# Down projection by seven products of half matrices in place of eight

## The chip, the cores and the metric

The kernel runs on one core of a Trainium2 chip. Five engines work side by side, each with an instruction queue of its own that it works off in order: PE (TensorE, matmuls), DVE (VectorE), ACT (ScalarE), POOL (GpSimd) and SP (SyncE, which here only issues DMAs). All data are f32. The metric is the device time of one execution in microseconds (us), median of three runs.

## The reference

The input x is 8 sequences of 512 tokens with 512 features. After a layer norm two branches run on each sequence. The first is a state space model (input projection, causal convolution of four taps, a scan with 16 states over 1024 channels, gating, output projection). The second is a gated feed-forward network whose gate is shifted by a low-rank term that an attention yields. The output is x + s * silu(g). What the change touches is the end of the second branch:

```python
gate_pre = h @ W_in_base.T + mod * (h @ A) @ B
gate = jax.nn.silu(gate_pre)
up = h @ W_up_base.T
mlp_out = gate * up @ W_down.T          # (512 x 2048) @ (2048 x 512), per sequence
return residual + mlp_out
```

The residual is the normalised x.

## The kernel before

**Two stages.** The first 640 us are the attention of all eight sequences (32 items: 8 sequences x 4 groups of heads). An order written out as a string of letters places each step; a table `const_steps` hangs small extra steps at given places (sequence, group, slot) of it. After that comes the scan stage, one sequence ("batch") after another, in which everything else happens: for batch b the scan, gate/up projections, down projection and z gates, for batch b - 1 the output projection, for batch b + 1 the input projection and convolution.

**The scan loop.** A batch has 64 iterations k, each with two chunks. An iteration holds a tile x of 128 x 1024 (two states of a channel block). It is loaded ahead by SP (`load_scan(k + 5)`, L650), multiplied by the input factor (`inputs`: on DVE for even k, L672, on POOL for odd k, L674), scanned in two halves on DVE (`scan_half`, L680, with the decays that ACT writes to PSUM, L658), multiplied by the output factor on POOL (`outputs`, L685), and summed over the states on PE (`sum_states`, L697, a burst of 16 instructions every four iterations).

**The work beside it.** The PE work of a batch is a list of parts (`batch_parts`), each with a number of units (one unit is a 512-column f32 matmul, which is two instructions), the weight tiles that it needs, and a function. `prefetch` has SP load weights up to `limits` minus one tiles ahead. In each chunk parts are issued until the share of units done has reached the share of chunks done. A part returns functions with a delay in chunks; `next_chunk` calls those that are due before the scan half of that chunk, and so they stand in DVE's, ACT's or POOL's queue at that place. The total is 300 units per batch.

**PSUM banks.** `bank` hands out four banks for matmul results in turn, two of a pool `ps_1` and two of a second pool.

**The down projection** stands last in the list of a batch, with z gates (`z_gate`, eight per batch) spread between. `down_proj(b, m)` makes output block m (128 features x 512 tokens) as one accumulation of 16 matmuls (L372) of 512 columns: the operand is `mlp[b, f]` (128 hidden features x 512 tokens), the weights are four tiles of 256 KB (`load_down`, L240). One chunk after its last part DVE adds the residual (L379, from the PSUM bank), ACT writes the tanh back to the bank (L380), and one chunk later DVE makes tanh and sum into twice the silu (L385, one input in PSUM). After the first block's parts `load_h(b + 1)` is issued: five DMAs on SP that bring the next batch's h into the tile `ht`, which has one buffer, and its modulation.

**What makes the operand.** `gate_up` computes four hidden blocks at a time (fq of 0 to 3, block 4 fq + i): gate (L310, L340) and then up, whose product with the gate (`up(i)`, L345) is the finished `mlp` tile. The first eight blocks are those of fq 0 and 1.

**The step size of the next batch** is a chain of small operations on DVE and ACT (`exponential`, `logarithm`, `softplus`, `scaled`, L556 to L594) that falls into the same stretch as the down projection.

Of the kernel before, what the change touches and what calls it, by code (L numbers as in the profile page):

```python
# [10 lines left out]
F32 = mybir.dt.float32  # L11
BF16 = mybir.dt.bfloat16
AF = mybir.ActivationFunctionType
ALU = mybir.AluOpType
# [4 lines left out]
P = 128  # L19
NB = 8  # L20
S = 512
DM = 512
KT = DM // P
TT = S // P
DI = 1024
ND = DI // P
# [3 lines left out]
HG = NH * HD // P  # L30
NF = 2048 // P
# [5 lines left out]
QD = 32  # L37
AHEAD = 5
SLOTS = TT * (TT + 1) // 2


@with_exitstack
def mamba_gated_ffn_kernel(
# [31 lines left out]
    scr_m = [dram.tile([R, S], F32, tag=f"scr_m{b}", name=f"scr_m{b}") for b in range(NB)]  # L75
    scr_c = [dram.tile([DI, S], F32, tag=f"scr_c{b}", name=f"scr_c{b}") for b in range(NB)]
    scr_r = [dram.tile([S], F32, tag=f"scr_r{b}", name=f"scr_r{b}") for b in range(NB)]
    scr_a = dram.tile([NS, P // NS, P], F32, tag="scr_a", name="scr_a")

    ident = const.tile([P, P], F32, tag="ident", name="ident")  # L80
# [12 lines left out]
    ctx.enter_context(tc.manual_schedule())  # L93


    banks = {"n": 0, "second": None, "special": None}

    def bank(name):
        if banks["special"]:
            return banks["special"](name)  # L100
        banks["n"] += 1
        pool = banks["second"] if banks["second"] and banks["n"] % 4 // 2 else ps_1
        return pool.tile([P, 512], F32, tag="mm", name=name)

    xnt, ht = {}, {}
# [5 lines left out]
    def load_h(b):  # L111
        ht[b] = act.tile([P, KT, S], F32, tag="ht", name=f"ht_{b}", bufs=1)
        nc.sync.dma_start(ht[b], scr_x[b][:, KT:, :])
        modh[b] = act.tile([4 * QD, S], F32, tag="modh", name=f"modh_{b}", bufs=1)
        for i in range(4):
            nc.sync.dma_start(modh[b][i * QD : i * QD + R, :], scr_m[b])
# [118 lines left out]
        nc.sync.dma_start(w, w_ffn[f][:, which])  # L235
        loaded["wgu", b, f, which] = w

    def load_down(b, m, q):
        w = wst.tile([P, NF // 4, P], F32, tag="wd", name=f"wd_{b}_{m}_{q}", bufs=4)
        nc.sync.dma_start(w, w_ffn[ts(q, NF // 4), :, 2, m, :].rearrange("f p c -> p f c"))  # L240
        loaded["wd", b, m, q] = w

    def load_out(b, m, q):
        w = wst.tile([P, ND // 2, P], F32, tag="wout", name=f"wout_{b}_{m}_{q}", bufs=3)
# [55 lines left out]
    def gate_up(b, fq):  # L300
# [42 lines left out]
        def up(i):  # L343
            m = mlp[b, 4 * fq + i]
            nc.vector.scalar_tensor_tensor(m, m, 0.5, st[i, 1], ALU.mult, ALU.mult)  # L345

        def second(i):
            product(i, 1, range(KT))
            return [(2, lambda: up(i))]

        def part(i, which, units, fn):
            p = units, [("wgu", lambda: load_gu(b, 4 * fq + i, which))], fn
# [6 lines left out]

    silus = {}  # L360

    def down_proj(b, m):

        st = {}

        def down(q):
            if q == 0:
                st["acc"] = bank(f"ps_acc_{b}_{m}")
            w = loaded.pop(("wd", b, m, q))
            for j in range(NF // 4):  # L370
                f = q * (NF // 4) + j
                nc.tensor.matmul(  # L372
                    st["acc"], lhsT=w[:, j, :], rhs=mlp[b, f], start=(f == 0), stop=(f == NF - 1)
                )
            return [(1, residual), (2, product)] if q == 3 else []

        def residual():
            f = tmp.tile([P, S], F32, tag="f", name=f"f_{b}_{m}", bufs=KT + 1)
            nc.vector.tensor_tensor(f, st["acc"], xnt[b][:, m, :], ALU.add)  # L379
            nc.scalar.activation(st["acc"], f, AF.Tanh, scale=0.5)  # L380
            st["f"] = f

        def product():
            f = st["f"]
            nc.vector.scalar_tensor_tensor(f, st["acc"], 1.0, f, ALU.add, ALU.mult)  # L385
            silus[b, m] = f

        return [
            (4, [("wd", lambda q=q: load_down(b, m, q))], lambda q=q: down(q)) for q in range(4)
        ]  # L390

    def finish(b, m):
# [45 lines left out]
    def finish_last(b, m):  # L438

        st = {}  # L440
        H = S // 2

        def out_proj(h, blocks):
            if "ps" not in st:
# [267 lines left out]
    def batch_parts(b):  # L712
# [23 lines left out]
        else:  # L736
# [1 line left out]
                parts += quads[i][0] + convs[2 * i] + quads[i][1][:2] + convs[2 * i + 1]  # L738
                parts += quads[i][1][2:]
            parts += sizes[0]  # L740
        for m in range(KT):
            down = down_proj(b, m)
            parts += down
            if m == 0 and b + 1 < NB:
                parts.append((0, [], lambda: load_h(b + 1)))
        total = sum(p[0] for p in parts) + 4 * ND
        done, out_, z = 0, [], 0
        for p in parts:
# [48 lines left out]
    with ExitStack() as c1:  # L797
# [272 lines left out]
        def turn(b, kt):  # L1070

            if kt == 0:
                xnT[b] = act.tile([P, KT, S], F32, tag="ht", name=f"xnT_{b}", bufs=1)
                xrT[b] = act.tile([P, KT, S], F32, tag="xnt", name=f"xrT_{b}")
            ps = bank(f"ps_x_{b}_{kt}")
            for tt in range(TT):
                nc.tensor.transpose(ps[:, ts(tt, P)], norm[b][tt][:, ts(kt, P)], ident)

            def evict():
                nc.scalar.copy(xnT[b][:, kt, :], ps)  # L1080
                nc.gpsimd.tensor_tensor(  # L1081
                    xrT[b][:, kt, :].rearrange("p (t c) -> p t c", t=TT),
                    xnT[b][:, kt, :].rearrange("p (t c) -> p t c", t=TT),
                    rms[b][1].rearrange("p (c t) -> p t c", t=TT), ALU.mult,
                )
                if kt == KT - 1:
                    nc.sync.dma_start(scr_x[b][:, :KT, :], xnT[b])

            return evict
# [213 lines left out]
        def started(parts):  # L1303
# [14 lines left out]
            [],  # L1318
        )

        const_steps = dict(zip(
            ((0, 0, 3), (0, 1, 2), (1, 0, 0), (1, 0, 1), (1, 1, 0), (1, 1, 1), (1, 1, 2), (1, 2, 1),
             (1, 2, 2)),
            constants(),
        ))
        sizes = step_size(0)

        spare = {}

# [323 lines left out]
```

## Time and profile before

Before: 2956.67 us, median of three runs (2955.38 to 2958.57).

| what | us |
|---|---|
| profiled execution | 2959.42 |
| its span, first to last instruction | 2957.6 |
| PE busy | 2916.1 |
| DVE busy | 2508.3 |
| POOL busy | 1983.2 |
| matmuls of the down projection (L372), 1024 instructions | 451.3 |
| scans on DVE (L680), 1024 | 1208.5 |
| output factor on POOL (L685), 512 | 1206.6 |
| granted PE clock, mean | 0.997 |

A group's line gives line, engine, operation, output <- inputs, shapes and count, then busy us and the mean ns of one, then the idle time of the engine before it and what ended it. PEld is the loading of weights, which runs beside PE's matmuls. A line of the chain gives the share of the span in which a line's work was what the end waited for. A line of stretches gives from:to, its length, then busy us and count of PE, PEld, DVE, ACT and POOL, the granted clock, the share of DMA and GB/s. A line of the timeline gives start, length, engine, line, operation.

### The profile page before, as it was taken

How to read it: one execution, taken by the hardware profiler on the slowest of the kernel's cores; microseconds unless marked ns; L12 is line 12 of the kernel's file. 1: busy time of each engine (PE TensorE's matmuls, PEld its weight loads, DVE VectorE, ACT ScalarE, POOL GpSimd, SP SyncE). 2: the span in 40 equal slices, each digit the busy share in tenths (PEclk: the TensorE clock that was granted, in tenths of full speed). 3: DMA queues.
4: the chain of work that ended last, by engine and by line, in shares of the span. 5: the costliest groups of instructions: out<-in, count | busy, mean ns of one | idle time of the engine just before them, and what ended most of it. 6: DMA issues, size and time to landing. Idle time of an engine off the chain costs nothing.

```text
span 2957.6 us, 33937 instructions
## 1 busy us (share of the span) xinstructions
PE 2916.1 (99%) x11440; PEld 1257.8 (43%) x11440; DVE 2508.3 (85%) x2855; ACT 1258.7 (43%) x2192; POOL 1983.2 (67%) x924
## 2 busy tenths in 40 slices
PE   9999999999999999999999999999999999999999
PEld 5544545444333443444444344434443444344434
DVE  5777777688998999799979987998799879988885
ACT  4555555443444344334433433443344334433332
POOL 3433333107889778777878777777778777878884
PEclk9999999999999999999999999999999999999999
DMA  4767777779887978797879787877787878788874
GB/s 162 196 188 192 194 194 195 202 201 220 213 198 204 236 202 204 201 232 195 201 197 230 198 202 193 231 202 203 187 234 187 208 186 241 190 209 200 209 195 114
DMA packets 316465, 595.00 MB, mean 201 GB/s; under 512 B 32605, under 2 KB 164317, under 8 KB 311684
## 3 DMA queue, kind: packets, MB, share of 16 engines
q1 hardware_dynamic: 310096, 576.31, 75.2%
q0 software_dynamic: 2192, 10.50, 1.0%
q10 hardware_dynamic: 4004, 6.01, 0.8%
q8 instruction: 92, 1.51, 0.2%
q14 instruction: 81, 0.66, 0.1%
HBM read 466.04 MB, written 42.77 MB: 172 GB/s over the span
## 4 chain that ended last, share of the span: by engine, by line
PE 90%; DVE 5%; ACT 1%; SPq 1%; DMA 1%; POOL 1%; issue 1%; DVEq 0%; POOLq 0%; ACTq 0%
PE ps_gu L310 30%; PE ps_acc L372 15%; PE ps_in L218 13%; PE y L697 8%; PE ps_out L401 7%; PE ps_q L1136 3%; PE s L1159 2%; PE ps_k L1136 2%; PE o_ps L1220 2%; DVE mx L1172 2%; DVE p L1196 1%; PE ps_z L1113 1%; PE ps_gu L321 1%; SPq L1205 1%; ACT p L1181 1%; PE s L1164 1%
## 5 line engine op out<-in xcount | busy, mean ns | idle before, releaser
L685 POOL TENSOR_TENSOR x<-x,cc 128x1024 f32<-128x1024 f32 x512 | 1206.6, 2364 | 451.6 <-DVE x L680 425.9
L680 DVE TENSOR_TENSOR_SCAN x<-decay,x 128x512 f32<-128x512 f32 x1024 | 1208.5, 1208 | 3.0 <-ACT decay L658 2.7
L658 ACT ACTIVATE decay<-dt,an 128x511 f32<-128x511 f32 x1024 | 695.3, 687 | 643.9 <-DVE x L680 627.0
L310 PE MATMUL ps_gu<-ht,wgu 128*128 128x512 f32 x2048 | 914.8, 598 | 0.0
L674 POOL TENSOR_TENSOR x<-x,bb 128x1024 f32<-128x1024 f32 x256 | 607.5, 2373 | 67.2 <-DMA wgu<-in_w_ffn 64.9
L310 PEld LDWEIGHTS ps_gu<-ht,wgu 128*128 128x128 f32 x2048 | 381.0, 190 | 521.7 <-issue 475.6
L372 PE MATMUL ps_acc<-m,wd 128*128 128x512 f32 x1024 | 451.3, 597 | 0.0
L218 PE MATMUL ps_in<-xnt,win 128*128 128x512 f32 x952 | 426.2, 594 | 0.0
L1181 ACT ACTIVATE p<-s,mx 128x256 f32<-128x256 f32 (+3 forms) x512 | 228.3, 528 | 193.7 <-DVE mx L1172 185.7
L672 DVE TENSOR_TENSOR x<-x,dtb_ps 128x1024 f32<-128x1024 f32 x255 | 304.6, 1194 | 1.1 <-ACT dtb_ps L669 0.5
L372 PEld LDWEIGHTS ps_acc<-m,wd 128*128 128x128 f32 x1024 | 192.2, 190 | 259.0 <-issue 250.8
L218 PEld LDWEIGHTS ps_in<-xnt,win 128*128 128x128 f32 x952 | 178.2, 190 | 221.5 <-issue 215.0
L1172 DVE TENSOR_REDUCE mx<-s 128x2 f32<-128x1024 f32 (+3 forms) x256 | 196.5, 808 | 76.0 <-PE s L1164 76.0
L697 PE MATMUL y<-x,sel 128*32 128x512 f32 x2048 | 251.2, 601 | 4.8 <-POOL x L685 4.8
L401 PE MATMUL ps_out<-xc,wout 128*128 128x512 f32 x496 | 219.4, 594 | 0.0
L1196 DVE STREAM_TRANSPOSE p<-p 128x2048 f32<-128x2048 f32 (+3 forms) x128 | 188.7, 1493 | 23.9 <-ACT p L1181 21.4
L257 DVE SCALAR_TENSOR_TENSOR conv<-ps_in,cw,conv 128x511 f32<-128x511 f32 x165 | 122.8, 745 | 42.2 <-ACT conv L276 38.3
L401 PEld LDWEIGHTS ps_out<-xc,wout 128*128 128x128 f32 x496 | 92.7, 190 | 118.8 <-issue 118.8
L1081 POOL TENSOR_TENSOR xrT<-xnT,rms 128x512 f32<-128x512 f32 x28 | 42.9, 1532 | 141.7 <-ACT xnT L1080 141.7
L1159 PE MATMUL s<-k,q 32*128 32x512 f32 (+3 forms) x1024 | 123.3, 480 | 8.8 <-ACT p L1181 8.0
L294 ACT ACTIVATE zth<-ps_in 128x512 f32<-128x512 f32 x64 | 38.2, 597 | 220.0 <-PE ps_in L218 220.0
L697 PEld LDWEIGHTS y<-x,sel 128*32 128x32 f32 x2048 | 54.3, 109 | 181.2 <-issue 145.5
(214 smaller groups left out, 2103.7 us busy)
## 6 DMA issues: line engine op xcount, KB each, us to landing
x<-scr_c SPq DMA_DIRECT2D x512, 512.0 KB, 6.7
pt<-p SPq DMA_DIRECT2D x512, 160.0 KB, 3.4
wgu<-in_w_ffn SPq DMA_DIRECT2D x256, 256.0 KB, 5.7
win<-in_w_in SPq DMA_DIRECT2D x128, 256.0 KB, 5.3
wd<-in_w_ffn SPq DMA_DIRECT2D x128, 256.0 KB, 5.1
scr_c<-xc SPq DMA_DIRECT2D x64, 256.0 KB, 3.7
wout<-in_out_w SPq DMA_DIRECT2D x64, 256.0 KB, 4.3
xt<-in_x SPq DMA_DIRECT2D x32, 256.0 KB, 4.3
```

The source lines that it names most:

```text
L218: nc.tensor.matmul(ps, lhsT=w[:, kt, :], rhs=xnt[b][:, kt, :], start=(kt == 0), stop=(kt == KT - 1))
L310: nc.tensor.matmul(st[i, which], lhsT=w[:, kt, :], rhs=ht[b][:, kt, :], start=(kt == 0), stop=(kt == KT - 1 and (which == 1 or i == 3)),)
L372: nc.tensor.matmul(st["acc"], lhsT=w[:, j, :], rhs=mlp[b, f], start=(f == 0), stop=(f == NF - 1))
L401: nc.tensor.matmul(st["ps"], lhsT=w[:, d % 4, :], rhs=xc[b, d], start=(d == 0), stop=(d == ND - 1),)
L658: nc.scalar.activation(decay[n][:, 1:], spread[b][2][:, 1:], AF.Exp, scale=an[:, g // 4, g % 4 : g % 4 + 1])
L672: nc.vector.tensor_tensor(t, t, by.unsqueeze(1).to_broadcast([P, 2, S]), ALU.mult)
L674: nc.gpsimd.tensor_tensor(t, t, spread[b][0].unsqueeze(1).to_broadcast([P, 2, S]), ALU.mult)
L680: nc.vector.tensor_tensor_scan(t, decay[n], t, 0.0, ALU.mult, ALU.add)
L685: nc.gpsimd.tensor_tensor(t, t, spread[b][1].unsqueeze(1).to_broadcast([P, 2, S]), ALU.mult)
L697: nc.tensor.matmul(y[ts(j, QD), :], lhsT=sel[:, i0 + n, :], rhs=xs[k - 3 + j][:, n, :], start=(i0 + n == 0), stop=(i0 + n == 3),)
L1172: nc.vector.reduce_max(mx[i], sc[i][:, :, :w], axis=AX.X, negate=True)
L1181: nc.scalar.activation(to[:, :, :, ts(h, QD)].rearrange("p b k i -> p k b i"), sc[h // 2][:, h % 2, :w].rearrange("p (k b i) -> p k b i", ...
```

## The change

The operand of the down projection (2048 hidden features x 512 tokens) and the weights are cut in halves both ways: hidden features into low (blocks 0 to 7) and high (8 to 15), tokens into FIRST and SECOND (256 each), output features into two pairs of blocks. The eight products of quarters become seven (Strassen's algorithm in the form with shared sums), in the order 1, 5, 6, 3, 7, 2, 4.

- **Weights.** Four of the seven take sums of weight quarters (`SUMS`). They are made once, in the attention, on POOL: at eight places `load_quarters` brings two tiles of 256 KB, and at the next item `sum_quarters` makes four 128 x 256 sums on POOL and stores them by four DMAs on SP to a scratch `scr_w`. The tiles are buffers of the tags `bb` and `cc`. The other three products take raw quarters of the weights. A batch now loads 28 tiles of 256 KB in place of 16; a part with one tile has two units in place of four, and the batch has 292 units.
- **Operand.** One difference per low block is made by POOL after `up(i)`, with a delay of four chunks (`halves`: SECOND - FIRST, 128 x 256). Three more per low block are made in place by DVE between the products (`turn`), 24 operations of 128 x 256 whose operands all lie in SBUF. One set of them goes to a tile `t2`, which takes the buffer of `ht`.
- **Matmuls.** 112 of 256 columns per batch in place of 64 of 512. They accumulate in two fixed banks p and q of `ps_1`; while they run `bank` hands out only the second pool. Products 6, 7 and 3 add to what 1 and 5 left in the bank.
- **Evictions.** After each product DVE adds the bank's two halves to the residual or to what is there (14 additions of 128 x 256 per batch in place of 4 of 128 x 512). The tanh goes to an SBUF tile `th`, so the product that follows has all its inputs in SBUF.
- **load_h(b + 1)** is issued with the second part of product 7, after the last reader of `t2`.

```diff
+SUMS = {5: 0, 6: 1, 7: 2, 3: 3}
+RAW = {1: (0, 0), 2: (1, 0), 4: (1, 2)}
...
-        pool = banks["second"] if banks["second"] and banks["n"] % 4 // 2 else ps_1
+        second = banks["down"] or banks["n"] % 4 // 2
+        pool = banks["second"] if banks["second"] and second else ps_1
...
+        def halves(i):
+            m = mlp[b, 4 * fq + i]
+            nc.gpsimd.tensor_tensor(m[:, SECOND], m[:, SECOND], m[:, FIRST], ALU.subtract)
+
         def second(i):
             product(i, 1, range(KT))
-            return [(2, lambda: up(i))]
+            return [(2, lambda: up(i))] + [(4, lambda: halves(i))] * (4 * fq + i < ND)
...
-    def down_proj(b, m):
+    H = S // 2
+    FIRST, SECOND = slice(0, H), slice(H, S)
+
+    def down_parts(b):
...
+        def turn(which, j):
+            low, high = mlp[b, j], mlp[b, NF // 2 + j]
+            t2 = st["t2"][:, ts(j, H)]
+            to, x, y = {
+                2: (t2, high[:, SECOND], low[:, SECOND]),
+                3: (low[:, FIRST], t2, low[:, FIRST]),
+                4: (low[:, SECOND], high[:, FIRST], t2),
+            }[which]
+            nc.vector.tensor_tensor(to, x, y, sub)
+
+        def evict(to, x, cols, bank_):
+            for i in range(2):
+                m = 2 * to + i
...
+                f = st[m, "f"][:, cols]
+                by = xnt[b][:, m, cols] if x else f
+                nc.vector.tensor_tensor(f, st[bank_][:, ts(i, H)], by, add)
+
+        def tanh(r):
+            for m in (2 * r, 2 * r + 1):
+                th = tmp.tile([P, S], F32, tag="th", name=f"fth_{b}_{m}", bufs=3)
+                nc.scalar.activation(th, st[m, "f"], AF.Tanh, scale=0.5)
+                st[m, "th"] = th
+
+        def product(r):
+            for m in (2 * r, 2 * r + 1):
+                f = st[m, "f"]
+                nc.vector.scalar_tensor_tensor(f, st[m, "th"], 1.0, f, ALU.add, ALU.mult)
+                silus[b, m] = f
...
+        def part(of, n):
+            i, q = divmod(n, 2)
...
+            for k in range(NF // 4):
+                j = 4 * q + k
                 nc.tensor.matmul(
-                    st["acc"], lhsT=w[:, j, :], rhs=mlp[b, f], start=(f == 0), stop=(f == NF - 1)
-                )
...
+                    ps[:, ts(i, H)], lhsT=w[:, k, :], rhs=operand(of, j),
+                    start=(of in (1, 5, 2) and n == 0 and k == 0),
+                    stop=(n == 3 and k == NF // 4 - 1), skip_group_check=True,
+                )
+            if of == 1 and n:
+                todo.append((1, lambda: turn(2, n - 1)))
+            elif of == 5:
+                todo += [(1, lambda j=j: turn(2, j)) for j in ((3,), (4,), (5,), (6, 7))[n]]
+            elif of in (6, 3):
+                todo += [(1, lambda j=j: turn(3 if of == 6 else 4, j)) for j in (2 * n, 2 * n + 1)]
+            elif of == 7 and n == 1 and b + 1 < NB:
+                load_h(b + 1)
+            if n == 3:
+                todo.append((1, ends[of]))
+                if of in (2, 4):
+                    r = of // 4
+                    todo += [(1, lambda: tanh(r)), (2, lambda: product(r))]
...
+        def sum_quarters(j):
...
+            nc.gpsimd.tensor_tensor(s1, a21, a22, ALU.add)
+            nc.gpsimd.tensor_tensor(s2, s1, a11, ALU.subtract)
+            nc.gpsimd.tensor_tensor(s3, a11, a21, ALU.subtract)
+            nc.gpsimd.tensor_tensor(s4, a12, s2, ALU.subtract)
...
+        for j in range(ND):
+            at = items_of(2 * HG + j)
+            const_steps[*at, 3] = lambda j=j: load_quarters(j)
+            at = items_of(2 * HG + j + 1)
+            const_steps[*at, 1] = lambda j=j: sum_quarters(j)
```

## The prediction

> **What bounds the kernel now.** I read the page's busy shares and its chain that ended last, then the stretches of one batch, then the groups of the lines that the change touches, and last the order of time around them.
>
> ```profile
> PE 2916.1 (99%) x11440; PEld 1257.8 (43%) x11440; DVE 2508.3 (85%) x2855; ACT 1258.7 (43%) x2192; POOL 1983.2 (67%) x924
> ...
> PE 90%; DVE 5%; ACT 1%; SPq 1%; DMA 1%; POOL 1%; issue 1%; DVEq 0%; POOLq 0%; ACTq 0%
> PE ps_gu L310 30%; PE ps_acc L372 15%; PE ps_in L218 13%; PE y L697 8%; PE ps_out L401 7%; PE ps_q L1136 3%; PE s L1159 2%; PE ps_k L1136 2%; PE o_ps L1220 2%; DVE mx L1172 2%; DVE p L1196 1%; PE ps_z L1113 1%; PE ps_gu L321 1%; SPq L1205 1%; ACT p L1181 1%; PE s L1164 1%
> ```
>
> PE carries the chain, and the down projection (L372) is 15% of it: work taken from PE pays, as long as no other engine takes the lead. The stretches of one batch say how near they are (the columns are PE, PEld, DVE, ACT and POOL busy; the first line is the down projection, the other two are the convolution stages).
>
> ```profile
> 1430.00:1500.00 70.00, 70.00 (x210) 28.69 (x209) 59.05 (x63) 26.39 (x41) 54.31 (x24) 1.00 0.81 208
> 1580.00:1650.00 70.00, 70.00 (x222) 28.22 (x221) 66.76 (x74) 30.04 (x48) 56.04 (x25) 1.00 0.90 236
> 1650.00:1720.50 70.50, 70.50 (x223) 27.65 (x222) 65.76 (x72) 29.33 (x47) 55.29 (x25) 1.00 0.75 191
> ```
>
> A batch repeats every 290.5 us (first weight load of L372 at 1139.4, 1429.9, 1720.5). In the 70 us of its down projection DVE has 11 us to spare. Now the pieces of the chain that price a matmul:
>
> ```profile
> 1430.53 6.87 PE ps_acc L372 x16
> ...
> 2945.48 3.47 PE ps_out L451 x16
> ```
>
> A 512-column instruction (a f32 matmul is two) takes 0.429 us. The last output projection already uses 256 columns (L451): 3.47/16 = 0.217, so halves nearly halve. Then the groups by shape, with the mean ns of one:
>
> ```profile
> L685 POOL TENSOR_TENSOR x<-x,cc 128x1024 f32<-128x1024 f32 x512 | 1206.6, 2364 | 451.6 <-DVE x L680 425.9 <-DVE sp L572 12.3 <-DMA x<-scr_c 11.8
> L379 DVE TENSOR_TENSOR f<-ps_acc,xnt 128x512 f32<-128x512 f32 x32 | 21.9, 684 | 46.1 <-PE ps_acc L372 46.1
> L594 DVE TENSOR_TENSOR bb<-bb,dt 128x512 f32<-128x512 f32 x7 | 13.2, 1890 | 1.1 <-DMA dt<-scr_p 1.1
> L574 DVE SCALAR_TENSOR_TENSOR sp<-sp 32x16 f32<-32x16 f32 x7 | 11.5, 1637 | 0.2
> L1253 DVE TENSOR_TENSOR mo<-ps_o,den 128x256 f32<-128x256 f32 x30 | 12.7, 425 | 1.8
> ```
>
> And the order of time around one L594:
>
> ```profile
> 1460.30 2.36 POOL L685 TENSOR_TENSOR x<-x,cc 128x1024 f32<-128x1024 f32 x1 [0.66 <-DVE x L680]
> 1461.25 1.96 DVE L594 TENSOR_TENSOR bb<-bb,dt 128x512 f32<-128x512 f32 x1
> 1462.13 0.37 SPq L240 DMA_DIRECT2D wd<-in_w_ffn  x1
> 1462.60 0.52 SPq L650 DMA_DIRECT2D x<-scr_c  x1
> 1462.61 2.81 POOL L674 TENSOR_TENSOR x<-x,bb 128x1024 f32<-128x1024 f32 x1
> ```
>
> This is the row that decides. L379 and L594 are the same operation at the same size; L379 has one input in PSUM and takes 0.684, L594 has both in SBUF and takes 1.89. It started 0.95 us into a GpSimd operation, ended 0.55 after that one, and GpSimd's next ran 0.45 longer than its usual 2.36. Even the 32x16 operation of L574 takes 1.64. So a DVE operation whose inputs are all in SBUF waits for the GpSimd operation under way, and reads as busy meanwhile. Nearly all large DVE work of the scan now has an operand in PSUM; the change adds 28 per batch that have not (24 differences in turn, 4 products whose tanh moves from PSUM to an SBUF tile).
>
> **The change, part by part.** *Matmuls.* Per batch 128 instructions of 512 columns (128 x 0.4294 = 55.0 us) become 224 of 256 (224 x 0.2169 = 48.6): 6.4 us saved, 51 in all. The bounds of the price are 0.214 (exact half) and 0.254 (8 of L1113's with 272 columns in 2.03 us); I take L451, the same shape with changing weights. Each load of weights, 190 ns, must fit under 217 where it had 429. The Trainium skill (TensorE: Matmul & The Clock Gate, section The mechanism) speaks against this: it says that a load of weights overlaps matmuls in flight only when it goes to another row group. By that rule each matmul would pay its 190 ns, 224 x 0.19 = 43 us more per batch. L451 decides otherwise: 16 pairs in 3.47 us leave no room for 16 x 0.19 in series.
>
> *DVE, without waits.* Work is paced by units: a batch has 300 of them over 128 chunks, now 292, so a part of two units is 0.877 chunk. A chunk costs DVE one scan (2.33 for two) and a quarter of L672 (1.14 net): 1.45. Of a 256-wide operation I count 0.34, as L1253's 0.425 less the 0.09 by which DVE operations overlap (L379 at 1447.76, 0.67 long, the next at 1448.34).
> Products 1, 5, 6, 3: 32 units and a z gate, 15.8 chunks: 22.9; the small chain of the next batch's step size (L556 to L594, with today's waits) 8.3; z and y 1.9; added 24 turns x 0.34 = 8.2 and 8 evictions 2.7. Sum 44.0. PE in the same parts: 128 x 0.2169 + 3.4 + two bursts of y at 1.85 = 34.9.
> Products 7, 2, 4: 28 units, 12.3 chunks: 17.8; z and y 2.5, 6 evictions 2.0, 4 products 2.4: 24.7. PE: 96 x 0.2169 + 3.4 + 2.8 = 27.0.
>
> *The waits.* Lower bound 0. Upper bound 2.1 each, what L574 shows in five batches of seven (2.22 less 0.16). Between them the order decides: GpSimd runs an output (L685) after the second scan of an even iteration, right behind it an input (L674), and an output after the odd one, 2.36 each. With one turn per chunk, the four turns of two iterations meet 1.3 (DVE's own multiply lies before), 1.2, 0 (it starts before GpSimd, as L572 mostly does) and 1.25: mean 0.94. With two per chunk the eight meet 1.3, 2.36, 0, 0, 0, 2.36, 0, 0: mean 0.75. So 8 x 0.94 + 16 x 0.75 = 19.4 us, and four products at 0.8, 3.2. L594's mean wait is 1.2, the first of a burst (L556, L562, L572, L594) 0.94, those that follow 0.4: 0.8 is in their middle. The Trainium skill (SBUF — State Buffer, section Who interferes with whom) has the second of the two engines blocked until the first has finished; read at its worst that is 2.36 for each of 28, 66 us per batch, where the rows here show a part of an operation.
>
> *Sum of a batch.* First four products: DVE 44.0 + 19.4 = 63.4 against PE's 34.9. PE can run ahead by product 7 at most (32 x 0.217 = 6.9) until it needs the eviction of product 3, and less where the load of ht (below) holds SP's queue: at least a part (1.7). I take 4. PE stalls 28.5 - 4 = 24.5. The other three: 24.7 + 3.2 - 27.0 = 0.9. Less the 6.4 saved: +19.0. Behind a waiting turn stand the scans, so the outputs on GpSimd and the y matmuls are late next, and product 6 on PE, which reads the turns. The last batch has no small chain and no load_h: 55.1 - 34.9 - 6.9 + 0.9 - 6.4 = +7.8. Seven and one: 140.8.
>
> *The rest.* In the convolution stages, with DVE busy 132.5 of 140.5, iterations come 2.7% denser: 2.4 us more of scans and inputs, still under PE; for the uneven places I take 1 per batch, 8 in all (bounds 0 and 2.4 x 8). GpSimd's eight subtractions per batch (256 of 1024 columns of L685: 0.6 each, 4.8) lie in the gate stage, where GpSimd is idle 26%; product 5 reads them some 40 us later. Uncovered: 38 in all. The sums in the attention: 32 operations at 0.6 on a GpSimd busy a third of it; in its queue they stand before normalise and the xrT multiplies, on SP's 16 loads and 32 stores stand before the moves of the probabilities, and the stores wait for the sums. The blocks of 20 us per item cover 2.4 us; I take 2 in all (bounds 0 and 20). The store to scratch is read only from the first down projection. load_h moves from the 16th of 64 units to after product 7's second part, with 5 DMAs (1 MB in 6.1 us, four of 8.3): on SP it waits for the last turn, and the loads of the weights and of the scan stand behind it; that is why the lead is 4 and not 6.9. ht itself is needed 17 us of PE later. Down's banks: p and q are free one product (6.9) ahead of reuse, against one chunk of 2.3.
> Sum: 140.8 + 8 + 2 = +151 us. The profiled execution took 2959.4 (span 2957.6 and 1.8 around it), so 3110; the median of the runs lies 2.7 lower: 3107.
>
> **The rivals.** *The saving arrives (faster).* The turns fall where GpSimd is idle (22% of the time; L573 is free in six batches of seven) and wait 0.1, and PE leads by product 7 and a z gate, 10.3. Then the stall is 46.4 - 34.9 - 10.3 = 1.2, a batch gains 5.2, the last 6.4: 2924. With that lead it decides below a wait of 0.26. Against it: DVE exceeds PE by 9 us there without any wait.
> *Long waits.* Each waits 1.26 as L594 in most batches: 74.2 - 34.9 - 4 + 2.7 - 6.4 = +31.6, the last +20.4: 3208. At 2.1 it would be 3397.
> *The weights come late.* 28 loads stand in place of 16, and three parts ahead now mean 5.2 us of PE against a median landing of 5.1 (up to 10.9). At 8 us a part takes 2.67: 74.7 for PE's 61.9, +6.4 per batch, if the turns cost nothing: 3018. For it: DMA is at 0.81 there. Against it: with DVE slower, parts take 3.3 and three ahead are 9.8.
> *Halves that don't halve.* At L1113's 0.254 the products take 56.9, nothing is saved, and PE binds: 2982.
>
> **How the numbers follow.** Chances: forecast 0.58, with a range of its own of 3041 to 3173 (waits of 0.5 and 1.1); the saving 0.13; long waits 0.12; late weights 0.11; no halving 0.06. The range 2965 to 3210 takes in the last two and most of the long waits and leaves out the saving and a tail above, 0.18 together. A measurement tells 0.2% from no change. Faster 0.13, same 0.03, slower 0.84.
>
> **What the profile after would show.** L372's successor at 0.217 per instruction (else the first step is wrong); the turns' mean well over 0.42 us, near 1.2; PE idle of some 20 us per batch ahead of product 6 and 7, released by DVE; a batch period near 309. If the turns take 0.42, or PE has no gaps, the forecast is wrong and the time is below 2957; if the gaps end with wd landing, the third rival holds.

## The result, and the profile after

The changed kernel takes 3114.86 us (median of four runs, 3113.71 to 3117.41) against 2956.03 for the kernel before on the same chip: a ratio of 1.0537, with an interval of 1.0519 to 1.0556. The forecast was 3107. The profiled execution took 3113.71, its span is 3111.9, 154.3 more than before.

The page, busy shares and chain, of the changed kernel:

```profile
PE 2918.0 (94%) x12208; PEld 1427.0 (46%) x12208; DVE 2711.8 (87%) x3127; ACT 1263.3 (41%) x2192; POOL 2056.1 (66%) x1020
...
PE 60%; DVE 25%; POOL 4%; issue 3%; DMA 3%; ACT 3%; SPq 2%; DVEq 0%; POOLq 0%; ACTq 0%
PE ps_gu L320 21%; PE ps_in L222 10%; DVE x L764 9%; PE ps_out L486 6%; PE y L781 5%; DVE m L401 4%; PE ps_q L1216 3%; POOL x L769 2%; DVE x L756 2%; PE s L1239 2%; PE ps_k L1216 2%; SPq L1285 2%; PE ps_acc_p L448 2%; DVE t L401 2%; PE ps_acc_q L448 2%
```

Two things are to be seen. DVE's part of the chain has gone from 5% to 25%, and its scans (L764) and turns (L401) are in it now: PE is no longer the only bound. And PE is busy 2918.0 us, no less than the 2916.1 before, although its matmuls should be 51 us shorter. The groups of the new lines say where that is from (L448 is the matmul of the seven products, L401 a turn, L410 an eviction, L359 the difference on GpSimd, L421 the product with the tanh):

```profile
L448 PE MATMUL ps_acc_q<-m,wd 128*128 128x256 f32 x768 | 185.6, 401 | 58.2 <-DMA wd<-in_w_ffn 28.1 <-DVE x L764 18.0 <-DVE f L410 12.1
L448 PE MATMUL ps_acc_p<-m,wd 128*128 128x256 f32 x768 | 179.1, 388 | 20.1 <-DVE f L410 17.7 <-DMA wd<-in_w_ffn 2.3
L448 PE MATMUL ps_acc_p<-t,wd 128*128 128x256 f32 x256 | 78.6, 465 | 34.2 <-DVE t L401 33.8 <-DMA wd<-scr_w 0.3
L401 DVE TENSOR_TENSOR m<-t,m 128x256 f32<-128x256 f32 x64 | 67.3, 1090 | 0.0
L401 DVE TENSOR_TENSOR t<-m,m 128x256 f32<-128x256 f32 x64 | 62.9, 993 | 0.0
L401 DVE TENSOR_TENSOR m<-m,t 128x256 f32<-128x256 f32 x64 | 57.1, 936 | 0.0
L359 POOL TENSOR_TENSOR m<-m 128x256 f32<-128x256 f32 x64 | 46.8, 735 | 0.0
L421 DVE SCALAR_TENSOR_TENSOR f<-fth,f 128x512 f32<-128x512 f32 x32 | 36.3, 1174 | 0.4 <-ACT fth L415 0.4
L410 DVE TENSOR_TENSOR f<-ps_acc_p,xnt 128x256 f32<-128x256 f32 x48 | 17.8, 410 | 4.0 <-PE ps_acc_p L448 4.0
```

A turn takes 1.006 us in the mean of its three forms, an eviction of the same size, with one input in PSUM, 0.41. The products are busy 443.3 us in all and stand idle 112.5 us ahead of their instructions, 14 per batch. Some of the busy time is a slower clock, as the order of time on PE in the third batch shows (start, length, then in brackets the idle time before and what ended it):

```profile
1500.97 5.34 PE L448 MATMUL ps_acc_q<-m,wd 128*128 128x256 f32 x24
...
1513.26 2.86 PE L448 MATMUL ps_acc_p<-t,wd 128*128 128x256 f32 x12
1517.85 0.70 PE L448 MATMUL ps_acc_p<-t,wd 128*128 128x256 f32 x2 [1.73 <-DVE t L401]
1520.34 7.11 PE L448 MATMUL ps_acc_p<-t,wd 128*128 128x256 f32 x18 [1.79 <-DVE t L401]
1527.29 7.07 PE L448 MATMUL ps_acc_q<-m,wd 128*128 128x256 f32 x32
1536.12 1.99 PE L448 MATMUL ps_acc_p<-m,wd 128*128 128x256 f32 x8 [1.76 <-DVE f L410]
...
1554.38 10.16 PE L448 MATMUL ps_acc_q<-m,wd 128*128 128x256 f32 x32 [9.04 <-DVE x L764]
...
1569.77 7.17 PE L448 MATMUL ps_acc_p<-m,wd 128*128 128x256 f32 x32
```

Undisturbed, 24 matmuls take 5.34 and 32 take 7.07 to 7.17, the 0.22 each that was forecast. But after the two short gaps of product 6 (L448 with operand t) 18 matmuls take 7.11, not 3.9, and after the 9.04 us ahead of product 2, 32 take 10.16. The stretches show DVE and the clock beside it (from:to, length, busy us and count of PE, PEld, DVE, ACT, POOL, then granted clock, DMA share, GB/s):

```profile
1488.00:1520.00 32.00, 28.82 (x128) 18.45 (x126) 31.65 (x39) 11.21 (x17) 21.33 (x9) 0.99 0.80 203
1520.00:1552.00 32.00, 23.25 (x98) 17.88 (x98) 31.97 (x39) 6.22 (x9) 14.71 (x7) 0.87 0.53 149
...
1520.30:1527.30 7.00, 6.96 (x19) 5.67 (x20) 7.00 (x9) 1.38 (x2) 3.36 (x2) 0.57 0.52 146
...
1554.30:1564.40 10.10, 10.02 (x33) 8.34 (x34) 5.12 (x7) 2.07 (x3) 9.44 (x5) 0.69 1.01 242
```

In the first 64 us DVE has no free time left (31.65 and 31.97 of 32), where before it had 11 free in 70; and the clock falls to 0.57 and 0.69 in just the two runs of slow matmuls. A DVE turn behind a GpSimd operation, in the order of time:

```profile
1537.77 1.21 DVE L764 TENSOR_TENSOR_SCAN x<-decay,x 128x512 f32<-128x512 f32 x1
...
1539.06 2.37 POOL L769 TENSOR_TENSOR x<-x,cc 128x1024 f32<-128x1024 f32 x1 [4.27 <-DVE x L764]
...
1540.01 4.85 DVE L401 TENSOR_TENSOR m<-m,t 128x256 f32<-128x256 f32 x4
1541.39 2.53 POOL L758 TENSOR_TENSOR x<-x,bb 128x1024 f32<-128x1024 f32 x1
1544.79 1.21 DVE L764 TENSOR_TENSOR_SCAN x<-decay,x 128x512 f32<-128x512 f32 x1
...
1545.92 0.73 DVE L401 TENSOR_TENSOR m<-m,t 128x256 f32<-128x256 f32 x2
```

The four turns from 1540.01, beside two GpSimd operations, take 4.85 in place of 1.6; the two at 1545.92, right behind a scan and with GpSimd idle, take 0.37 each.

Last, the gap of 9.04 us. The trace lays it to DVE, but the instruction of DVE that it names is a scan which product 2 does not read. The instructions of SP show what it was (start, length, line):

```profile
1534.39 0.32 SPq L250 DMA_DIRECT2D wd<-scr_w  x1
1546.68 0.32 SPq L117 DMA_DIRECT2D ht<-scr_x  x1
1547.05 1.81 SPq L120 DMA_DIRECT2D modh<-scr_m  x4
1548.96 0.40 SPq L250 DMA_DIRECT2D wd<-in_w_ffn  x1
```

SP stands for 12 us at load_h, which may start only when the last turn has read the buffer, and the weights of product 2 (`wd<-in_w_ffn`) are issued behind it. The DMA engines are busy at 0.53 in that stretch, and at 0.20 from 1536.0 to 1545.3, while SP stands. Product 2 starts 5.4 us after its weights are issued.

Over the whole span the difference stands as follows. The first y matmul, where the scan stage begins, is at 722.97, against 700.84: 22 us are lost in the attention. From the first y to the last it is 2360.7, against 2228.9: 132 more. From the second batch to the seventh a batch repeats every 304 to 308 us (290.5), its down projection takes 83 to 87 (70.0).

### The profile page after: what moved, and what is told of

Its sections match the earlier page's. It is cut to its first block, busy times and chain, and to the rows that moved or that the text cites. A ratio compares the mean times of both kernels' runs of the same rounds, so it can differ in the third digit from the quotient of the medians.

```text
span 3111.9 us, 36122 instructions
## 1 busy us (share of the span) xinstructions
PE 2918.0 (94%) x12208; PEld 1427.0 (46%) x12208; DVE 2711.8 (87%) x3127; ACT 1263.3 (41%) x2192; POOL 2056.1 (66%) x1020
## 4 chain that ended last, share of the span: by engine, by line
PE 60%; DVE 25%; POOL 4%; issue 3%; DMA 3%; ACT 3%; SPq 2%; DVEq 0%; POOLq 0%; ACTq 0%
PE ps_gu L320 21%; PE ps_in L222 10%; DVE x L764 9%; PE ps_out L486 6%; PE y L781 5%; DVE m L401 4%; PE ps_q L1216 3%; POOL x L769 2%; DVE x L756 2%; PE s L1239 2%; PE ps_k L1216 2%; SPq L1285 2%; PE ps_acc_p L448 2%; DVE t L401 2%; PE ps_acc_q L448 2%
## 5 line engine op out<-in xcount | busy, mean ns | idle before, releaser
L764 DVE TENSOR_TENSOR_SCAN x<-decay,x 128x512 f32<-128x512 f32 x1024 | 1208.6, 1206 | 2.9 <-ACT decay L742 2.7
L781 PE MATMUL y<-x,sel 128*32 128x512 f32 x2048 | 259.4, 603 | 15.9 <-POOL x L769 15.9
L448 PE MATMUL ps_acc_q<-m,wd 128*128 128x256 f32 x768 | 185.6, 401 | 58.2 <-DMA wd<-in_w_ffn 28.1
L448 PE MATMUL ps_acc_p<-m,wd 128*128 128x256 f32 x768 | 179.1, 388 | 20.1 <-DVE f L410 17.7
L448 PEld LDWEIGHTS ps_acc_q<-m,wd 128*128 128x128 f32 x768 | 154.3, 203 | 89.8 <-DVE f L410 23.7
L448 PEld LDWEIGHTS ps_acc_p<-m,wd 128*128 128x128 f32 x768 | 145.4, 193 | 66.7 <-issue 22.5
```

Of the source, the lines that this page charges most:

```text
L448: nc.tensor.matmul(ps[:, ts(i, H)], lhsT=w[:, k, :], rhs=operand(of, j), start=(of in (1, 5, 2) and n == 0 and k == 0), stop=(n == 3 and k ...
L764: nc.vector.tensor_tensor_scan(t, decay[n], t, 0.0, ALU.mult, ALU.add)
L781: nc.tensor.matmul(y[ts(j, QD), :], lhsT=sel[:, i0 + n, :], rhs=xs[k - 3 + j][:, n, :], start=(i0 + n == 0), stop=(i0 + n == 3),)
```

## The experiments

The down stage is the time from the first matmul of the down projection to the next gate/up matmul; the period is the time from one down stage to the next. Both are given for the second to the seventh batch. Ratios are to the kernel before; first y is the start of the scan stage in the profiled execution.

| run | median us | ratio, interval | first y | down stage | period |
|---|---|---|---|---|---|
| before | 2956 | 1 | 700.8 | 70.0 | 290.5 |
| after | 3114.86 | 1.0537, 1.0519 to 1.0556 | 723.0 | 83 to 87 | 304 to 308 |
| e1 load_h late | 3080.81 | 1.0425, 1.0409 to 1.0441 | 723.0 | 76 to 80 | 299 to 302 |
| e2 turns from PSUM | 2999.90 | 1.0150, 1.0135 to 1.0165 | 720.4 | 70 to 73 | 291 to 294 |
| e3 sums alone | 2978.78 | 1.0078, 1.0063 to 1.0093 | 721.4 | 70.0 | 290.5 |
| e4 stores from GpSimd | 3114.39 | 1.0536, 1.0518 to 1.0553 | 722.9 | 83 to 88 | 304 to 309 |
| e5 turns on GpSimd | 3079.17 | 1.0418, 1.0403 to 1.0434 | 721.2 | 76 to 82 | 299 to 305 |
| e6 e1 and e2 together | 2988.50 | 1.0109, 1.0092 to 1.0126 | 724.5 | 66 to 71 | 287 to 292 |
| e7 sums' DMAs on GpSimd | 3110.05 | 1.0521, 1.0504 to 1.0537 | 722.1 | 83 to 87 | 304 to 308 |
| e9 turns spread on DVE | 3104.67 | 1.0498, 1.0478 to 1.0517 | 721.1 | 81 to 86 | 304 to 309 |
| e10 GpSimd's sums only | 2955.84 | 1.0004, 0.9995 to 1.0014 | 701.3 | 70.0 | 290.5 |
| e11 sums' DMAs only | 2963.55 | 1.0028, 1.0017 to 1.0039 | 707.4 | 70.0 | 290.5 |
| e12 e6 with half the weight loads | 2964.84 | 1.0033, 1.0021 to 1.0046 | 724.4 | 63 to 65 | 286 to 288 |
| e13 before, 256 columns | 2957.33 | 1.0013, 1.0004 to 1.0022 | 699.4 | 70.3 | 290.8 |

**e1: load_h behind the last weights.** Only its place is changed, from the second part of product 7 to the third of product 2.

```diff
-            elif of == 7 and n == 1 and b + 1 < NB:
+            elif of == 2 and n == 2 and b + 1 < NB:
                 load_h(b + 1)
```

> The changed kernel (3115) with one move: the five DMAs that bring the next batch's h are issued with the third part of product 2 in place of the second part of product 7; the rest is as it is. Theory A (SP's queue stands still behind this load until DVE's last turn, the loads of the weights behind it come late, and PE waits some 8 to 9 us ahead of product 2 in each of seven batches): the gap ahead of product 2 goes, 3115 - 7 x 6 to 8 = 3060 to 3075. Theory B (DVE alone is the bound there, the gap only moves to the next wait for a turn or an eviction): 3105 to 3120.

It gains 34 us and lies between the two theories, nearer to A. The third batch's product 2 on PE:

```profile
1545.35 7.17 PE L448 MATMUL ps_acc_q<-m,wd 128*128 128x256 f32 x32 [2.03 <-DVE f L410]
```

The gap of 9.04 has become 2.03, and without it the 32 matmuls run at the full clock, 7.17 in place of 10.16. The gaps of product 6 are as in the changed kernel (1.72 and 1.79, ended by the turns). So SP's queue did cost what the gap showed, about 6 us per middle batch (period 299 in place of 305), but DVE's lag remains.

**e2: the same turns with one operand in PSUM.** Each of the three forms takes one of its inputs from a bank (`dtb_ps`) and not from SBUF; number, size and order of the instructions stay.

```diff
-                2: (t2, high[:, SECOND], low[:, SECOND]),
-                3: (low[:, FIRST], t2, low[:, FIRST]),
-                4: (low[:, SECOND], high[:, FIRST], t2),
+                2: (t2, high[:, SECOND], dtb_ps[:, FIRST]),
+                3: (low[:, FIRST], t2, dtb_ps[:, FIRST]),
+                4: (low[:, SECOND], dtb_ps[:, FIRST], t2),
```

> The changed kernel with one of the two SBUF inputs of each of the 24 turns replaced by a tile in PSUM of the same size (dtb_ps), so the differences are of other data and the down projection's values are not the reference's; count, size, place and order of all instructions stay. Theory A (a DVE operation whose inputs are all in SBUF waits for GpSimd's operation under way): the turns fall from a mean of 1.0 us to 0.41, DVE is ahead by 14 us per batch, load_h is let go earlier, and the time falls by 9 to 14 us per batch, to 3003 to 3043. Theory B (the turns' own work and the place of load_h make the loss, the waits are covered): 3090 to 3115, turns at 0.41 all the same.

The groups of the turns:

```profile
L401 DVE TENSOR_TENSOR t<-m,dtb_ps 128x256 f32<-128x256 f32 x64 | 24.8, 396 | 0.0
L401 DVE TENSOR_TENSOR m<-t,dtb_ps 128x256 f32<-128x256 f32 x64 | 23.2, 399 | 0.0
L401 DVE TENSOR_TENSOR m<-dtb_ps,t 128x256 f32<-128x256 f32 x64 | 23.0, 404 | 0.0
```

0.40 in place of 1.006: the wait was 0.6 for each, 116 us over the kernel's 192, and the scan stage is 113 us shorter. DVE stands idle 0.0 ahead of the turns in both kernels, so it is not a wait for data that the edit has taken away. Theory A holds: the second SBUF operand of 24 small operations is what most of the loss in the scan stage hangs on. The trace also shows what the waits had covered:

```profile
1493.52 3.69 PE L448 MATMUL ps_acc_q<-m,wd 128*128 128x256 f32 x16 [1.18 <-DMA wd<-scr_w]
1498.20 3.72 PE L448 MATMUL ps_acc_q<-m,wd 128*128 128x256 f32 x16 [0.99 <-DMA wd<-scr_w]
...
1513.42 9.15 PE L448 MATMUL ps_acc_q<-m,wd 128*128 128x256 f32 x32 [2.15 <-DMA wd<-in_w_ffn]
```

Now the gaps end with weights that land. That is the third rival, which could not be seen as long as DVE was later.

**e6: e1 and e2 together**, with the DMAs of the sums moved to GpSimd's queue (the edit of e7).

> The turns with one input from PSUM (of other data, so the down projection's values are not the reference's), load_h at the third part of product 2, and the loads and stores of the weights' sums on GpSimd's queue: what is left when all three causes found so far are away. Theory A (they are additive, and then PE binds): 3000 less 22 in the attention less some 20 of load_h: 2950 to 2965; theory C (the weights of the seven products then come late, 28 loads with three parts ahead, as gaps of 0.6 to 2.2 us show already): 2962 to 2985.

2988.50, above both ranges: the attention was not recovered (first y at 724.5). The scan stage is 2234.6, 13 us shorter than in e2, so load_h is worth 2 to 3 us per batch once the turns do not wait, where it was worth 6 while they did. Of the 30.3 us of gaps that are left in its products, 23.6 end with the weights and 6.5 with turns.

**e12: e6 with each weight tile loaded by half**, and that half used twice.

```diff
-        nc.sync.dma_start(w, src)
+        nc.sync.dma_start(w[:, :2, :], src[:, :2, :])
...
-                    ps[:, ts(i, H)], lhsT=w[:, k, :], rhs=operand(of, j),
+                    ps[:, ts(i, H)], lhsT=w[:, k % 2, :], rhs=operand(of, j),
```

> The kernel without the three causes found (turns with one input from PSUM, load_h late, the sums' transfers on GpSimd's queue; 2988) and in it each weight tile of the seven products loaded to half, each half used twice: half the weights are left out, all instructions on the engines stay. Theory C (what keeps the saving on PE from showing is that 28 loads per batch come late): the stretch of the seven products falls from 66 to 70 us to 62 to 65, 2950 to 2968. Theory A (DVE's own work keeps the time): 2982 to 2990.

The scan stage is another 23 us shorter than in e6, as theory C has it. The fourth batch on PE has products without a gap:

```profile
1767.74 7.17 PE L448 MATMUL ps_acc_p<-t,wd 128*128 128x256 f32 x32
1774.75 7.07 PE L448 MATMUL ps_acc_q<-m,wd 128*128 128x256 f32 x32
```

The down stage is 63.4 to 65.3, against 70.0 - 6.4 = 63.6, and the period 285.9 in the mean of the third to the sixth batch, below the 290.5 of before. So the seven products save 4.6 of the 6.4 us per batch that they should when the turns do not wait, load_h stands last and half of the weight traffic is gone. The time of 2964.84 has the 22 us of the attention in it; 2943 without them is an estimate, no run.

**e3: the sums of the weights alone**, put into the kernel before; nobody reads them.

```diff
+        def load_quarters(j):
...
+        def sum_quarters(j):
...
+        for j in range(ND):
+            at = items_of(2 * HG + j)
+            const_steps[*at, 3] = lambda j=j: load_quarters(j)
+            at = items_of(2 * HG + j + 1)
+            const_steps[*at, 1] = lambda j=j: sum_quarters(j)
```

> The kernel before (2956) with only the weights' sums in the attention, made and stored to scratch and read by nobody; the down projection is the old one. What the prediction had: +2 us. Theory A (the stores of the sums stand on SP ahead of the moves of the probabilities and wait there for GpSimd, which itself waits up to 14 us for another store; PE then waits for the moved probabilities): +18 to +24 us, all of it before the scan starts, 2974 to 2980. Theory B (the later start of the scan in the changed kernel comes from something else, as the changed banks or the longer program): 2956 to 2960.

It costs 22.8 us, as much as the changed kernel loses in the attention. The waits of this run in the attention (engine, line, what it waited for; total, times, longest), one of PE's and one of SP's:

```profile
PE o_ps L1221 <- DMA scr_w<-ws: 21.3, 2, 10.8
...
SPq L1356 <- POOL ws L1350: 26.5, 2, 13.6
```

Two waits of PE, 21.3 us, are nearly all of it. How they come about is seen on GpSimd's queue in the changed kernel, in the order of time (L1184 normalises, L1426 to L1429 make a sum each):

```profile
252.48 6.19 POOL L1184 TENSOR_SCALAR xnT<-xrT,ln 128x512 f32<-128x512 f32 x4 [14.57 <-DMA scr_x<-xnT]
258.98 0.63 POOL L1187 DMA_DIRECT2D scr_x<-xnT  x1 [0.30 <-POOL xnT L1184]
259.63 0.74 POOL L1426 TENSOR_TENSOR ws<-wq,wq 128x256 f32<-128x256 f32 x1
```

The sums of this place stand behind a normalisation that waits 14.57 us for a store. The kernel before had that wait too, and no wait of PE came of it:

```profile
POOL xnT L1104 <- DMA scr_x<-xnT: 98.0, 7, 14.8
```

Now SP stands at the store of the sums, issues it at 260.40, and behind it are the moves of the probabilities (`pt<-p`), which the matmul of L1300 reads. The trace lays PE's wait to the store, which that matmul does not read:

```profile
260.40 3.15 SPq L1432 DMA_DIRECT2D scr_w<-ws  x4
...
266.19 10.05 SPq L1285 DMA_DIRECT2D pt<-p  x16
...
280.08 4.23 PE L1300 MATMUL o_ps<-pt,z 128*32 128x256 f32 x48 [11.57 <-DMA scr_w<-ws]
...
364.86 4.49 PE L1300 MATMUL o_ps<-pt,z 128*32 128x256 f32 x48 [11.16 <-DMA scr_w<-ws]
```

It happens at two of the eight places, 11.57 + 11.16 = 22.7. At the other six PE has no such wait.

**e10 and e11: GpSimd's part and the traffic apart**, each in the kernel before. e10 has the 32 operations of e3 on tiles that are there, with no DMA; e11 has the loads and stores of e3 with no additions, and stores what it loaded.

> The kernel before (2956) with only GpSimd's part of the weights' sums in the attention: the same 32 operations at the same places, on data that lie in SBUF already, nothing loaded or stored, and nobody reads them. With loads and stores it was 2979. Theory A (the loads and stores cost, in the DMA queues and on SP): 2955 to 2959. Theory B (GpSimd's time, or what it is waited for, costs): 2968 to 2980.

> The kernel before with only the transfers of the weights' sums in the attention: the 16 loads and 32 stores on SP at the same places, the loaded tiles stored as they are, no operation on GpSimd and nobody reads them. Theory A (the traffic itself lengthens the moves of the probabilities, 1 MB more per item): 2970 to 2980. Theory B (only SP's wait for GpSimd costs, which is gone here): 2956 to 2963.

GpSimd's work alone costs nothing that can be measured (1.0004, 0.9995 to 1.0014). The traffic alone costs 8 us (its ratio of 1.0028 is 1.0017 to 1.0039), which lies between the theories. The other 14 of e3's 23 arise only when both are there, and e3's trace has SP waiting for GpSimd at the stores then. The parts do not simply add: e11 has none of the two long waits, but three for its stores of 4.2 us together.

**e4 and e7: the sums' DMAs off SP.** e4 issues the stores from GpSimd, e7 the loads too (in `load_quarters` and `sum_quarters`).

```diff
-                nc.sync.dma_start(
+                nc.gpsimd.dma_start(
                     scr_w[k, :, q, :, f, :].rearrange("i p c -> p i c"),
```

> The changed kernel with the 32 stores of the weights' sums issued from GpSimd's queue, right behind the sums, in place of SP's. Theory A (SP is held by these stores): the attention loses 16 to 22 us, 3093 to 3099. Theory B (GpSimd's own time or the DMA traffic is what costs): 3110 to 3120.

> The changed kernel with the loads as well as the stores of the weights' sums issued from GpSimd's queue; with the stores alone there the time stayed at 3114 and SP waited at the loads instead, whose buffers the late sums hold. Theory A (SP is held by either of the two, and with it the moves of the probabilities): the attention is back to its length before, 3090 to 3097. Theory B (the DMA traffic or GpSimd's own time costs): 3108 to 3118.

Neither recovers it. In e4 SP waits one step further on, at the loads of the next place, whose buffers the late sums still read:

```profile
SPq L1416 <- POOL ws L1428: 28.8, 2, 14.9
```

In e7 SP has none of them, and PE waits all the same, now for the moves of the probabilities themselves:

```profile
PE o_ps L1300 <- DMA pt<-p: 14.6, 4, 4.8
```

Between 200 and 400 us, where the sums are made, such a move lands after 4.6 us in the median, against 3.5 in the changed kernel. Why they land later when the sums' DMAs come from GpSimd's queue is left open.

**e5 and e9: the turns spread, one per part.** In both, the turns of product 6 and 3 are distributed to the parts of products 6, 3, 7 and 2, load_h stands at the second part of product 4, and the sums' DMAs are GpSimd's. e5 makes the turns on GpSimd, so that they wait for nobody but their queue; e9 makes them on DVE.

```diff
-            nc.vector.tensor_tensor(to, x, y, sub)
+            nc.gpsimd.tensor_tensor(to, x, y, sub)
...
-                todo += [(1, lambda j=j: turn(3 if of == 6 else 4, j)) for j in (2 * n, 2 * n + 1)]
+                todo.append((1, lambda: turn(3, n + 4 * (of == 3))))
+            elif of in (7, 2):
+                todo.append((1, lambda: turn(4, n + 4 * (of == 2))))
```

> The changed kernel with three moves: the 24 turns are made by GpSimd in place of DVE and spread one per part over products 1, 5, 6, 3, 7 and 2 (those for product 4 over 7 and 2); load_h is issued with the second part of product 4; the loads and stores of the weights' sums are issued from GpSimd's queue. Nothing is left out. Theory A (the turns' work and waits on DVE, the held SP queue in the scan and in the attention make the whole loss): DVE loses 24 us per batch, the PE saving of 51 us appears less some late weights, 2920 to 2970. Theory B (GpSimd, with 24 x 0.73 = 17.5 us more per batch in a stretch where it has 28 us of 35 already, becomes the bound): 2990 to 3040, with DVE and PE waiting for its inputs and outputs.

> As the kernel with the turns on GpSimd, spread one per part, but with the turns left on DVE. Theory A (waits for GpSimd decide, and they are no fewer when the turns stand alone: 0.94 against 0.75 each by the order of the operations): turns at 1.1 to 1.4 us, 3030 to 3065. Theory B (the loss came from the pile of two turns per chunk in products 6 and 3 and from load_h): 2970 to 3020.

Both missed their ranges on the slow side. The waits of PE in the scan stage of e5:

```profile
PE ps_gu L320 <- DMA ht<-scr_x: 42.5, 5, 9.4
PE ps_acc_p L448 <- POOL t L401: 35.5, 15, 4.1
```

On GpSimd a turn takes 0.73 to 0.79, and product 6 waits for them as it did for DVE's; 42.5 us go to a load_h that is now too late for the next batch's gate, which was a fault of the place I gave it. In e9 the turns take 1.0 to 1.29, no less than when they come two at a time, and the run is 24 us slower than e1. From the first to the last matmul of the seven products e9 takes 76 to 78 us and e1 76 to 80 in the same batches, so that spreading the turns brings no gain shows there; the change of load_h's place makes the times of the two runs a poor measure of it.

**e13: the price of half the columns.** The kernel before, with each matmul of its down projection in two of 256 columns.

```diff
-                nc.tensor.matmul(
-                    st["acc"], lhsT=w[:, j, :], rhs=mlp[b, f], start=(f == 0), stop=(f == NF - 1)
-                )
+                for h in range(2):
+                    nc.tensor.matmul(
+                        st["acc"][:, ts(h, S // 2)], lhsT=w[:, j, :],
+                        rhs=mlp[b, f][:, ts(h, S // 2)], start=(f == 0 and h == 0),
+                        stop=(f == NF - 1), skip_group_check=True,
+                    )
```

> The kernel before with each matmul of the down projection cut into two of 256 columns, with the weights loaded for each: 256 instructions of 256 columns per batch in place of 128 of 512, all else as it was. By the prediction's price of 0.217 against 0.429: 55.5 us per batch in place of 55.0, 2956 to 2964. By the third price weighed there (0.254): +10 per batch, 3030 to 3045.

Pieces of the chain (start, length, instructions):

```profile
1436.76 14.01 PE ps_acc L373 x64
...
1491.22 7.10 PE ps_acc L373 x32
```

14.01/64 = 0.219 with a load of weights for each, and 0.3 us more per batch (290.8). So the first step of the sum, the price of a matmul, holds.

## Why the prediction was right or wrong

**The sign and the mechanism** were right: DVE operations with both inputs in SBUF wait for GpSimd, DVE becomes the bound of the down projection, and PE's saving is lost behind it. e2 shows it by taking the waits away and nothing else: 113 of the 132 us lost in the scan stage go with them. The Trainium skill (SBUF — State Buffer, section Who interferes with whom) names the same pair of engines; the size is this case's own.

**The size of the wait** was 0.60 in the runs, in the place of 0.8: 24 x 0.2 = 4.8 us per batch too much. (The prediction's 8 x 0.94 + 16 x 0.75 is 19.5, where it has 19.4.) The product with the tanh (L421) takes 1.174 for 0.6 of work, a wait of 0.57 where 0.8 was taken; the operation takes 1.05 in e2 and 1.79 in e12, so its wait depends on the place.

**PE's price** of 0.217 was right (e13, and 0.22 in every undisturbed run of matmuls). So the rival of halves that don't halve falls. The sentence of the Trainium skill (TensorE: Matmul & The Clock Gate, section The mechanism) that a load of weights overlaps matmuls only in another row group does not hold for these f32 matmuls: e13 has one load of 190 ns for each matmul of 0.219. The same section names a second case, a load into a background weight buffer, which the prediction left out.

**The stall on PE** was forecast as 24.5 over the first four products, some 20 of it ahead of products 6 and 7, after a lead cut from 6.9 to 4 for load_h. That step failed in its parts. Ahead of 6 and 7 the third batch has 1.73 + 1.79 + 1.76 = 5.3; the largest gap, 9.04, is ahead of product 2. I had seen that SP's queue stands behind load_h, but priced it as 2.9 us of lead; e1 shows 6 per batch. With load_h away, the gaps of the products in e1, from their three groups' idle time, are (26.6 + 13.2 + 33.3)/8 = 9.1 per batch, and 12.5 with the slower clock of the next paragraph, where 25.4 was forecast. So DVE's lag was oversized by 13: 4.8 by the waits, 2.9 by the lead, and some 5 that the runs do not divide.

**The clock** was no term of the sum. The matmuls of the seven products are busy 443.3 us after, 409.5 in e12, where PE hardly waits: 34 us, 4 per batch, are put down to the lower granted clock (27 in e1, 3.4 per batch); in the third batch the two runs of slow matmuls above make 6 of them. This, and 8 us more in the y matmuls (259.4 against 251.2), is why PE's busy time did not fall. The forecast of the batch as a whole, +20, came near the measured 14 to 18 because the oversized lag covered the missing clock and the undersized queue.

**The weights that come late** were given as a rival, with +6.4 per batch if the turns cost nothing. e2, e6 and e12 show that it was a second layer and no alternative: with the turns' waits and load_h out of the way the period is 289.3 (mean of e6's four middle batches), and half of the traffic less makes it 285.9. So late weights cost at least 3.4 per batch; the down stage with half of them is 63 to 65.

**The layers in order**, by the mean period of the same four batches: 305.3 after; 291.9 without the turns' waits (-13.4); 289.3 with load_h late as well (-2.6); 285.9 with half the weights (-3.4); against 290.5 before and 284.1 by the saving alone. The order matters: load_h alone, taken first, is worth 6.

**The attention** was taken at 2 us, between bounds of 0 and 20; it cost 22, above the bound. I had listed each piece, the stores of SP that wait for sums and stand ahead of the probabilities, and then judged them by the cover of a 20 us block. What I had not looked up is where in GpSimd's queue the sums would stand: at two places behind a wait of 14.6 us that the trace of before shows, and that no one needed then. That this queue is the whole cause is not shown: in e7 SP does not stand behind it, and the 22 us stay. **The dense stages** were taken at 8 us in all. A middle batch without its down stage is 305.3 - 84.2 = 221.1, against 220.5, so 0.6 each; but the stretch between the last two down stages is 6.6 longer (195.8 against 189.2), and all that lies outside the down stages is some 13 longer. The last batch, taken at +7.8, lost 13.3 in its products (83.6 against 70.3).

So the total was hit by errors of both signs: 149 forecast for the scan stage and 132 measured, 2 for the attention and 22 measured. That 3107 lies within 8 us of 3115 is luck in this part; the sign and the cause are not.

No version that does all of the work with the seven products comes near the kernel before: the best, e5 and e1, take 3079 and 3081.

## What to carry to other kernels

Before matmuls are traded for elementwise work, price that work on its engine with the operands where they will lie: one SBUF operand more took an operation of 0.40 us to 1.0 here, on an engine that had 11 us free in 70. A step that is put into an in-order queue is as late as the longest wait ahead of it, even one that cost nothing till then, and whoever waits for that step hands the delay to the next queue. And where one bound hides another, take them away together: here the late weights could not be seen until the turns no longer waited, and load_h was worth 6 us per batch before that and 2.6 after.

## What the runs showed of the hardware that I had not expected

The granted clock can fall after short gaps, and the fall can cost nearly as much as the gaps. In the third batch two gaps of 1.73 and 1.79 us with 0.70 us of matmuls between them were followed by 7.0 us at 0.57, which made 18 matmuls 3.2 us longer; the gap of 9.04 was followed by 10.1 us at 0.69, 3.0 longer. In the same batch a single gap of 1.76 was followed by 9.3 us at 1.00. In e1 a gap of 2.03 was followed by 7.3 us at 1.00, in e2 one of 2.15 by 9.1 us at 0.81: the length of the gap alone does not decide it, and what does is not shown. The Trainium skill (TensorE: Matmul & The Clock Gate, section What's actually happening) puts the half rate after an idle window of about 3.4 us and the full rate after a busy one of the same length. The gaps of 1.73 and 1.79 are shorter than that. By an estimate from the page's half rate, a mean of 0.57 over 7.0 us means 6.0 us of it, so this run shows the fall sooner and the return later than the page has it.

The wait between DVE and GpSimd may go both ways: GpSimd's operation at 1541.39, next to the turns, took 2.53, where the mean of its group is 2.39, and 2.37 in e2, whose turns do not wait. In sum that is little, 6 us over the kernel.
